# Diagonal score blocks of 384 and 128 columns joined into one of 512, in two attentions of a hybrid network

## The chip, the cores and the metric

The kernel runs on one core of one Trainium2 chip. The metric is the device time of one execution in microseconds (us). A core has five engines that run their own instruction queues side by side: PE (TensorE, matrix products; PEld is its weight load), DVE (VectorE), ACT (ScalarE), POOL (GpSimd) and SP (SyncE, which here only issues transfers). PE writes to PSUM, 8 banks of 512 fp32 columns on 128 partitions; DVE and ACT read from there, POOL works on SBUF only.

## The reference

Two layers of a residual network over x of shape 4 x 1024 x 128, all fp32. Layer 0: gated linear attention, a mixture of experts, causal attention, the mixture again. Layer 1: rotary attention without softmax, a dense network, ALiBi attention, the dense network again. The change touches the two softmax attentions alone. Both have 16 heads of 8 columns, and T = 1024:

```python
def _L0_attn_b_ref(x, Wq, Wk, Wv, Wo):          # causal; values have 64 columns a head
    q = (x @ Wq).reshape(B, T, 16, 8).transpose(0, 2, 1, 3)      # k alike, v with 64
    scores = jnp.einsum('bhqd,bhkd->bhqk', q, k) / sqrt(8)
    scores = jnp.where(causal, -jnp.inf, scores)
    attn = jax.nn.softmax(scores, axis=-1)
    ctx = jnp.einsum('bhqk,bhkd->bhqd', attn, v)
    return ctx.transpose(0, 2, 1, 3).reshape(B, T, 16 * 64) @ Wo
def _L1_attn_b_ref(x, W_attn, b_attn, W_proj, b_proj, temperature):   # ALiBi; values have 8
    att = jnp.einsum('bqhd,bkhd->bhqk', q, k) * scale / temperature
    att = att + jnp.where(causal, slopes * rel, -jnp.inf)
    w = jax.nn.softmax(att, axis=-1)
    return jnp.einsum('bhqk,bkhd->bqhd', w, v).reshape(B, T, 128) @ W_proj + b_proj
```

## The kernel before, in words

The layers follow each other: gated linear attention, experts, causal attention (from about 360 to 1330 us of the profile), experts, rotary attention and the first dense layer, ALiBi attention (about 1690 to 2340), the second dense layer.

Both attentions run through `softmax_attention` (from L786). A number `n` stands for a pair of heads of one batch item: the queries and keys of one head lie on partitions 0 to 63 and those of the other on 64 to 127 (`g` is 0 or 1), and the pair's products use the two halves of PE. There are 8 pairs in a batch item, 32 in all. `Pairs.load` brings a pair in with SP's transfers, `Pairs.product` (L722) multiplies queries and keys, and `Pairs.hide` (L728) adds a large negative triangle to a 128 x 128 block on the diagonal with two more matmuls.

**Maxima.** For every query the largest score is needed before the exponential. `Pairs.maxima` makes scores with queries on partitions, in tiles of 128 queries (`i`) by up to 512 keys (`c` is 0 or 1), one PSUM bank a head, and DVE reduces each: with the mask (L750, followed by the read of its accumulator) where the tile reaches the diagonal, plainly (L755) where it does not. The list `BY_QUERY` has twelve such steps for a pair. At the end `least` joins the halves, and `finish` turns it (L764), splits it into `nm_hi` and `nm_lo` (L766, L768), and writes them by transfers into two rows of the queries, so that the next scores come out with the maximum subtracted. This runs ahead of the rest by two pairs and six steps.

**Rounds, steps and turns.** The main loop takes two pairs a round, 16 rounds in an attention. In a round it goes through `BY_KEY`, twelve steps: for each half of the queries (`c`), the key tiles `j`, 4 for the first half and 8 for the second. In the last four key tiles of a half the block lies on the diagonal, and only 512, 384, 256 and 128 queries remain. A step has two turns, one for each pair. A turn makes the scores of both heads in one tile of two banks (L722, L728), takes their exponential on ACT into an `e` tile (L853), and then issues one step of the maxima, one part of the products of the step before, and one item of the queue `later` (`some()`). Every third turn it also issues one piece of what is put beside the attention (in the causal one the routing of the next mixture).

**Causal attention.** The products (L972) add into two banks `o0` and `o1`, one in each turn of a step, since the values have 64 columns. POOL adds the exponentials of all key tiles into the first one, `e_first` (L990). After the last key tile of a half, `consume` queues in `later`: the sums of `e_first` (L1002), four reciprocals (L1010), the scaling of both parts on POOL (L1016), an empty turn, and the projection (L936); the values of the next four heads come in between (L921). PSUM: 4 single banks, one scores tile of two banks, and `o0`, `o1`. There are four `e` tiles and four `e_first` tiles.

**ALiBi attention.** The products (L1198) add into one bank, all in the second turn of a step; a column of ones in the values gives the sums, so that POOL adds nothing. `later` gets an empty turn and the division (transposes L1212, then L1215 and L1216 on DVE). PSUM: 3 single banks, two scores tiles of two banks, and `o`.

All this goes through a scheduler that places every instruction in its engine's queue and sets the waits; each engine then works its queue in that order.

Of the kernel before, what the change touches and what calls it, by code (L numbers as in the profile page):

```python
# [13 lines left out]
F32 = mybir.dt.float32  # L14
# [624 lines left out]
class Pairs:  # L639
# [93 lines left out]
    def maxima(self, n, pool, steps):  # L733
# [5 lines left out]
        for i, c in steps:  # L739
            cols = min(512, (i + 1) * P - 512 * c)  # L740
            for g in range(2):
                ps = k.bank()
                self.product(
                    ps[:, :cols], n, g, slice(i * P, (i + 1) * P), slice(512 * c, 512 * c + cols),
                    "q", False,
                )
                to = nm[:, c, g, i : i + 1]
                if i < 4 * (c + 1):
                    junk = pool.tile([P, 512], F32, tag="junk", name="junk", bufs=1)
                    nc.vector.tensor_tensor_reduce(  # L750
                        junk[:, :cols], ps[:, :cols], self.mask[:, 512 - cols :], -1.0, 3e38,
                        ALU.add, ALU.min, to,
                    )
                else:
                    nc.vector.tensor_reduce(to, ps[:, :cols], AX.X, ALU.max, negate=True)  # L755
            yield
# [25 lines left out]
BY_QUERY = [(i, c) for i in range(NB) for c in range(i // 4 + 1)]  # L782
BY_KEY = [(c, j) for c in range(2) for j in range(4 * c + 4)]


def softmax_attention(  # L786
# [41 lines left out]
    for first in range(0, count, 2):  # L828
        if first % per == 0 and first // per + 1 < B:
            before(first // per + 1)  # L830
        if first % per == 2 and first // per + 1 < B:
            prologue(first // per + 1)
        for n in (first + 4, first + 5):
            if n < count:
                pairs.load(n)
        for c, j in BY_KEY:
            start = max(j * P, c * 512)
            w = (c + 1) * 512 - start
            es = []
            for i in range(2):  # L840
                n = first + i
                ps = ps_e.tile([P, 2, 512], F32, tag="scores", name="scores")
                for g in range(2):
                    pairs.product(
                        ps[:, g, :w], n, g, slice(start, start + w), slice(j * P, (j + 1) * P), "k", True,
                        j < 4 * c,
                    )
                if j >= 4 * c:
                    for g in range(2):
                        pairs.hide(ps[:, g, :P], g)  # L850
                tag = "e_first" if hold and j == 0 else "e"
                e = work.tile([P, 2, 512], F32, tag=tag, name=tag)
                power = nc.scalar.activation(e[:, :, :w], ps[:, :, :w], AF.Exp, scale=scale)  # L853
                k.mark = [power.ins.name]
                es.append(e)
                next(ahead, None)
                if late is not None:
                    later.extend(late[i]() or ())
                some()
                turn += 1  # L860
                if beside and turn % 3 == 0:
                    beside.popleft()()
            late = consume(first // per, first % per // 2, c, j, es)
# [8 lines left out]
def causal_attention(k: Core, pairs: Pairs, wq_d, wk_d, wv_d, wo_d, bring, after):  # L872
# [5 lines left out]
    with (  # L878
# [78 lines left out]
        def consume(b, r, c, j, es):  # L957
            skip = max(j - 4 * c, 0) * P
            if j == 0:
# [6 lines left out]
            end = j == 4 * c + 3  # L966
# [3 lines left out]
            def product(which):  # L970
                for i in range(4):
                    nc.tensor.matmul(  # L972
                        outs[which][32 * i : 32 * i + 32, skip:],
                        lhsT=v[:, j, i, 32 * which : 32 * which + 32],
                        rhs=es[i // 2][:, i % 2, : 512 - skip],
                        start=(j == 0), stop=end, skip_group_check=True,
                    )
# [6 lines left out]
            def second():  # L984
                product(1)

                if j:
                    for i in range(2):
                        to = total[i][:, :, skip:]
                        nc.gpsimd.tensor_add(to, to, es[i][:, :, : 512 - skip])  # L990
                if c == 0 and j == 0:
                    nb, nr = divmod(b * 4 + r + 1, 4)
                    if nb < B:
                        return values(nb, nr)
# [23 lines left out]
                todo = [sums, *(partial(invert, t) for t in range(4)), scaled, lambda: None]  # L1018
# [107 lines left out]
def alibi_attention(k: Core, pairs: Pairs, weights: AlibiWeights):  # L1126
# [3 lines left out]
    with (  # L1130
# [54 lines left out]
        def consume(b, r, c, j, es):  # L1185
            skip = max(j - 4 * c, 0) * P
            end = j == 4 * c + 3
            if j == 0:
# [7 lines left out]
            def second():  # L1196
                for i in range(4):
                    nc.tensor.matmul(  # L1198
                        o[32 * i : 32 * i + 32, skip:],
                        lhsT=v[:, j, 4 * r + i, :],  # L1200
                        rhs=es[i // 2][:, i % 2, : 512 - skip],
                        start=(j == 0), stop=end, skip_group_check=True,
                    )
# [578 lines left out]
```

## Time and profile before

| | |
|---|---|
| three runs | 2537.66, 2547.32, 2554.1 us; median 2547.32 |
| profiled execution | 2547.5 us; its span, from first to last instruction, 2545.8 us |
| granted PE clock, mean | 0.92 |
| causal attention, first to last exponential | 360.9 to 1299.2 us |
| ALiBi attention, first to last exponential | 1698.9 to 2326.3 us |
| exponentials (L853) | 704 + 64 into `e_first`, half in each attention |
| additions into `e_first` (L990) | 320, 541.1 us of POOL |
| masked and plain maxima (L750, L755) | 1024 and 512, 496.6 and 330.2 us of DVE |

A row of the timeline has the start, the length, the engine, the line and operation, what is written and from what, the shape, and how many equal instructions follow each other; in brackets stands how long the engine had been idle and what ended it. Matmuls overlap, so the length of one is more than the distance to the next. A row of the waits has who waited for whom, the time in total, how often, and the longest.

### The profile page before, as it was taken

How to read it: one execution, taken by the hardware profiler on the slowest of the kernel's cores; microseconds unless marked ns; L12 is line 12 of the kernel's file. 1: busy time of each engine (PE TensorE's matmuls, PEld its weight loads, DVE VectorE, ACT ScalarE, POOL GpSimd, SP SyncE). 2: the span in 40 equal slices, each digit the busy share in tenths (PEclk: the TensorE clock that was granted, in tenths of full speed). 3: DMA queues.
4: the chain of work that ended last, by engine and by line, in shares of the span. 5: the costliest groups of instructions: out<-in, count | busy, mean ns of one | idle time of the engine just before them, and what ended most of it. 6: DMA issues, size and time to landing. Idle time of an engine off the chain costs nothing. (4 is left out here: it accounts for less than half of the span.)

```text
span 2545.8 us, 39865 instructions
## 1 busy us (share of the span) xinstructions
PE 2252.5 (88%) x14101; PEld 1237.0 (49%) x14101; DVE 1664.2 (65%) x4795; ACT 1254.0 (49%) x2033; POOL 927.2 (36%) x722
## 2 busy tenths in 40 slices
PE   6785679999999989998984999989999999997998
PEld 4564533443434344443343666744445444444666
DVE  6978265767657766776334776476777767774544
ACT  6553214455444544553431566615555555555865
POOL 2212405677488748766752332311001000000222
PEclk8988769999889989998997999967999999998999
DMA  9300230200200120100033000402113131000000
GB/s 255 111 9 17 85 105 22 80 19 26 84 26 19 40 77 23 31 18 27 2 98 98 9 9 1 131 2 89 35 34 111 34 101 45 24 24 1 9 9 18
DMA packets 92391, 124.80 MB, mean 49 GB/s; under 512 B 13211, under 2 KB 66462, under 8 KB 92174
## 3 DMA queue, kind: packets, MB, share of 16 engines
q1 hardware_dynamic: 88862, 115.76, 16.0%
q0 software_dynamic: 2560, 5.30, 0.6%
q8 instruction: 120, 1.97, 0.3%
q10 hardware_dynamic: 752, 0.98, 0.1%
q14 instruction: 97, 0.79, 0.1%
HBM read 67.57 MB, written 52.85 MB: 47 GB/s over the span
## 5 line engine op out<-in xcount | busy, mean ns | idle before, releaser
L853 ACT ACTIVATE e<-scores 128x1024 f32<-128x1024 f32 (+3 forms) x704 | 545.3, 792 | 583.8 <-PE scores L728 295.0
L990 POOL TENSOR_TENSOR e_first<-e_first,e 128x1024 f32<-128x1024 f32 (+3 forms) x320 | 541.1, 1722 | 327.1 <-ACT e L853 261.4
L750 DVE CUSTOM_DVE_ANT_0 junk<-bank,mask 128x128 f32<-128x128 f32 (+3 forms) x1024 | 496.6, 485 | 202.7 <-PE bank L722 134.2
L755 DVE TENSOR_REDUCE nm<-bank 128x1 f32<-128x512 f32 x512 | 330.2, 680 | 146.6 <-PE bank L722 144.4
L972 PE MATMUL o<-e,v 128*32 128x512 f32 (+3 forms) x2560 | 305.7, 497 | 0.0
L722 PE MATMUL bank<-aa_k,aa_q 62*128 62x512 f32 (+3 forms) x768 | 244.6, 427 | 26.1 <-DVE nm L755 15.7
L722 PE MATMUL bank<-ca_k,ca_q 62*128 62x512 f32 (+3 forms) x768 | 191.1, 419 | 31.0 <-DMA ca_k<-ca_k 13.9
L1198 PE MATMUL o<-e,v 128*32 128x512 f32 (+3 forms) x1536 | 218.2, 514 | 0.0
L722 PE MATMUL scores<-ca_q,ca_k 64*128 64x512 f32 (+3 forms) x768 | 181.3, 444 | 27.7 <-ACT e L853 26.0
L722 PEld LDWEIGHTS scores<-ca_q,ca_k 64*128 64x128 f32 x768 | 78.0, 188 | 250.1 <-ACT e L853 157.5
L728 PE MATMUL scores<-halves 64*128 64x128 f32 x2048 | 199.2, 261 | 0.0
L728 PEld LDWEIGHTS scores<-halves 64*128 64x128 f32 x2048 | 192.2, 195 | 11.1 <-issue 3.9
L722 PE MATMUL scores<-aa_q,aa_k 64*128 64x512 f32 (+3 forms) x768 | 171.3, 415 | 4.8 <-ACT e L853 4.7
L722 PEld LDWEIGHTS bank<-aa_k,aa_q 62*128 62x128 f32 x768 | 119.0, 199 | 108.1 <-DVE nm L755 60.0
L1108 POOL TENSOR_TENSOR lo<-val,hi 128x512 fp32r<-128x512 f32 x16 | 20.2, 1278 | 391.8 <-ACT hi L1107 372.2
L1516 DVE TENSOR_TENSOR h<-val,h 128x512 fp32r<-128x512 f32 x128 | 90.9, 718 | 102.8 <-ACT h L1515 77.1
L1470 PE MATMUL bank<-h,ff_h1s 128*128 128x512 f32 x512 | 135.5, 409 | 15.4 <-POOL h L1464 10.5
L1460 POOL CAST h<-gate 128x512 fp32r<-128x512 f32 x32 | 26.7, 834 | 333.2 <-DVE gate L1493 323.5
L722 PEld LDWEIGHTS scores<-aa_q,aa_k 64*128 64x128 f32 x768 | 80.2, 192 | 138.5 <-ACT e L853 63.9
L1010 DVE RECIPROCAL raw<-raw 128x128 f32<-128x128 f32 x128 | 117.6, 935 | 44.2 <-ACT raw L1006 44.2
L722 PEld LDWEIGHTS bank<-ca_k,ca_q 62*128 62x128 f32 x768 | 94.6, 200 | 99.5 <-issue 38.6
L1510 ACT ACTIVATE val<-bank,ff_t 128x512 f32<-128x512 f32 x128 | 88.2, 689 | 84.4 <-PE bank L1470 73.9
(291 smaller groups left out, 3716.6 us busy)
## 6 DMA issues: line engine op xcount, KB each, us to landing
aa_q<-aa_q SPq DMA_DIRECT2D x64, 208.0 KB
ca_q<-ca_q SPq DMA_DIRECT2D x64, 128.0 KB
ca_k<-ca_k SPq DMA_DIRECT2D x64, 128.0 KB
aa_k<-aa_k SPq DMA_DIRECT2D x64, 128.0 KB
wi<-in_moe_wi_dram SPq DMA_DIRECT2D x16, 256.0 KB
wo<-in_moe_wo_dram SPq DMA_DIRECT2D x16, 256.0 KB
back<-blank SPq DMA_DIRECT2D x8, 512.0 KB
got<-back SPq DMA_DIRECT2D x8, 512.0 KB
```

Of the source, the lines that this page charges most:

```text
L722: self.k.nc.tensor.matmul(out, lhsT=lhsT, rhs=rhs, start=True, stop=stop, skip_group_check=True)
L728: self.k.nc.tensor.matmul(ps, lhsT=part[:, 0, :], rhs=part[:, 1, :], start=False, stop=(a == 1), skip_group_check=True,)
L750: nc.vector.tensor_tensor_reduce(junk[:, :cols], ps[:, :cols], self.mask[:, 512 - cols :], -1.0, 3e38, ALU.add, ALU.min, to,)
L755: nc.vector.tensor_reduce(to, ps[:, :cols], AX.X, ALU.max, negate=True)
L853: power = nc.scalar.activation(e[:, :, :w], ps[:, :, :w], AF.Exp, scale=scale)
L972: nc.tensor.matmul(outs[which][32 * i : 32 * i + 32, skip:], lhsT=v[:, j, i, 32 * which : 32 * which + 32], rhs=es[i // 2][:, i % 2, : 512 ...
L990: nc.gpsimd.tensor_add(to, to, es[i][:, :, : 512 - skip])
L1010: nc.vector.reciprocal(part, part)
L1198: nc.tensor.matmul(o[32 * i : 32 * i + 32, skip:], lhsT=v[:, j, 4 * r + i, :], rhs=es[i // 2][:, i % 2, : 512 - skip], start=(j == 0), sto ...
L1470: nc.tensor.matmul(ps, lhsT=weights[:, c, :], rhs=inputs[c][i], start=(s == 0), stop=(s == len(steps) - 1))
L1510: nc.scalar.activation(val, ps, AF.Gelu, scale=s[:, o : o + 1])
L1516: nc.vector.tensor_sub(nxt[1][:, o, :], val, hi.bitcast(F32))
```

## The change

The lists of steps are rewritten. In the main loop the key tiles with 384 and 128 queries (the second and fourth of a diagonal) become one step: both blocks lie side by side in one scores tile, 512 columns a head, and one exponential covers them. The tile with 256 queries comes before them. A round has ten steps (20 turns) instead of twelve (24). In the maxima the tiles with 128 and 384 keys are joined alike, in one bank, and a pair has ten steps instead of twelve; both banks of a step are now asked for before the first matmul. The products, the additions on POOL and the maxima on DVE are still issued once for each block. The queue `later` gives two items in a turn while more than eight wait, and between the scaling and the projection stand two empty turns instead of one.

```diff
@@ Pairs.maxima
-        for i, c in steps:
-            cols = min(512, (i + 1) * P - 512 * c)
+        for c, several in steps:
+            parts, at = [], 0
+            for i in several:
+                cols = min(512, (i + 1) * P - 512 * c)
+                parts.append((i, cols, slice(at, at + cols)))
+                at += cols
+            banks = [k.bank() for _ in range(2)]
+            for i, cols, place in parts:
+                for g in range(2):
+                    self.product(
+                        banks[g][:, place], n, g, slice(i * P, (i + 1) * P), slice(512 * c, 512 * c + cols),
+                        "q", False,
+                    )
             for g in range(2):
-                ps = k.bank()
-                self.product(ps[:, :cols], n, g, ...)
-                to = nm[:, c, g, i : i + 1]
-                ... (one masked or plain reduction)
+                for i, cols, place in parts:
+                    to, ps = nm[:, c, g, i : i + 1], banks[g][:, place]
+                    ... (the same reduction, of ps)
             yield
@@
-BY_QUERY = [(i, c) for i in range(NB) for c in range(i // 4 + 1)]
-BY_KEY = [(c, j) for c in range(2) for j in range(4 * c + 4)]
+BY_QUERY = [
+    *((0, i) for i in ((0, 2), (1,), (3,), (4,), (5,), (6,), (7,))),
+    *((1, i) for i in ((4, 6), (5,), (7,))),
+]
+BY_KEY = [(c, j) for c in range(2) for j in [*((j,) for j in range(4 * c + 1)), (4 * c + 2,), (4 * c + 1, 4 * c + 3)]]
@@ softmax_attention
-        for c, j in BY_KEY:
-            start = max(j * P, c * 512)
-            w = (c + 1) * 512 - start
+        for c, several in BY_KEY:
+            parts, w = [], 0
+            for j in several:
+                skip = max(j - 4 * c, 0) * P
+                parts.append((j, skip, slice(w, w + 512 - skip)))
+                w += 512 - skip
...
-                for g in range(2):
-                    pairs.product(ps[:, g, :w], n, g, slice(start, start + w), ...)
-                if j >= 4 * c:
-                    for g in range(2):
-                        pairs.hide(ps[:, g, :P], g)
+                for j, skip, place in parts:
+                    for g in range(2):
+                        pairs.product(
+                            ps[:, g, place], n, g, slice(c * 512 + skip, (c + 1) * 512),
+                            slice(j * P, (j + 1) * P), "k", True, j < 4 * c,
+                        )
+                    if j >= 4 * c:
+                        for g in range(2):
+                            pairs.hide(ps[:, g, place.start : place.start + P], g)
...
-                some()
+                some(2 if len(later) > 8 else 1)
...
-            late = consume(first // per, first % per // 2, c, j, es)
+            late = consume(first // per, first % per // 2, c, parts, es)
@@ causal_attention, consume
             def product(which):
-                for i in range(4):
-                    nc.tensor.matmul(..., rhs=es[i // 2][:, i % 2, : 512 - skip], start=(j == 0), stop=end, ...)
+                for j, skip, place in parts:
+                    for i in range(4):
+                        nc.tensor.matmul(
+                            ..., rhs=es[i // 2][:, i % 2, place], start=(j == 0), stop=(j == 4 * c + 3), ...
+                        )
...
-                if j:
-                    for i in range(2):
-                        to = total[i][:, :, skip:]
-                        nc.gpsimd.tensor_add(to, to, es[i][:, :, : 512 - skip])
+                for i in range(2):
+                    for j, skip, place in parts:
+                        if j:
+                            to = total[i][:, :, skip:]
+                            nc.gpsimd.tensor_add(to, to, es[i][:, :, place])
...
-                todo = [sums, *(partial(invert, t) for t in range(4)), scaled, lambda: None]
+                todo = [sums, *(partial(invert, t) for t in range(4)), scaled, lambda: None, lambda: None]
@@ alibi_attention, consume: second() loops over parts in the same way
```

## The prediction

> **What bounds the kernel now.** I read the windows of the two attentions first, then the engines' timelines inside one undisturbed round of each, then the waits. The page gives the time of this execution and its fullest engine; the windows stand in pairs, one round and the whole attention, first the causal one, then ALiBi (columns: stretch, its length, PE, PEld, DVE, ACT, POOL busy, granted clock, DMA).
>
> ```profile
> span 2545.8 us, 39865 instructions
> PE 2252.5 (88%) x14101; PEld 1237.0 (49%) x14101; DVE 1664.2 (65%) x4795; ACT 1254.0 (49%) x2033; POOL 927.2 (36%) x722
> ```
>
> ```profile
> 783.30:832.40 49.10, 48.73 (x401) 21.12 (x398) 35.25 (x104) 24.73 (x37) 38.60 (x26) 1.00 0.06 17
> 360.90:1299.20 938.30, 883.67 (x6369) 377.83 (x6369) 601.98 (x1740) 440.58 (x658) 639.44 (x407) 0.94 0.12 34
> 2121.20:2157.50 36.30, 34.48 (x268) 17.24 (x266) 27.09 (x90) 19.75 (x28) 0.00 (x0) 1.00 0.17 39
> 1698.90:2326.30 627.40, 596.79 (x4375) 305.42 (x4377) 441.09 (x1435) 334.68 (x477) 19.73 (x14) 0.95 0.19 51
> ```
>
> ACT, whose instructions the change removes, is about half busy in both. The causal round has two parts. From the sums' end (787.0) to the end of the product that reads e_first in the second half (806.3), 19.3 us, PE's blocks follow each other without a gap. From there POOL runs without a gap until it has added everything the next sums need:
>
> ```profile
> 806.36 16.39 POOL L990 TENSOR_TENSOR e_first<-e_first,e 128x1024 f32<-128x1024 f32 x7 [5.65 <-ACT e L853]
> 822.70 2.52 POOL L1016 TENSOR_TENSOR ctx<-raw 128x512 f32<-128x512 f32 x2
> 825.16 8.41 POOL L990 TENSOR_TENSOR e_first<-e_first,e 128x1024 f32<-128x1024 f32 x5
> ```
>
> The sums already feel it; they take 1.74 us where POOL is last and 1.04 where it isn't (PE's timeline):
>
> ```profile
> 785.31 1.74 PE L1002 MATMUL bank<-e_first,ones 128*32 128x512 f32 x8
> ...
> 811.35 1.04 PE L1002 MATMUL bank<-e_first,ones 128*32 128x512 f32 x8
> ```
>
> In the ALiBi round POOL does nothing. PE and DVE hold each other through three PSUM banks: over that attention (first two rows) DVE waits 98.6 us for maxima matmuls; the third row, from the waits of the causal one, is the price of late POOL additions.
>
> ```profile
> DVE nm L755 <- PE bank L722: 69.3, 78, 2.7
> DVE junk L750 <- PE bank L722: 29.3, 56, 1.2
> ACT e L853 <- POOL e_first L990: 82.0, 37, 5.0
> ```
>
> **The change, part by part.** Durations are starts to next starts in the timelines of these rounds, clock 1.00.
>
> *Fewer exponentials.* ACT goes from 24 to 20 exponentials in each of 32 rounds, 128 fewer. The groups by form give the fixed part: 1026 ns for 1024 columns and 384 for 256 make 642 ns for 768, so 170 ns without columns; 128 x 0.17 = 21.8 us of ACT. It lies beside PE and DVE, so I count nothing; were ACT the bound it would be -22.
>
> ```profile
> L853 ACT ACTIVATE e<-scores 128x1024 f32<-128x1024 f32 x320 | 319.0, 1026 | 218.8 <-PE scores L722 111.8 <-PE scores L728 82.8 <-POOL e_first L990 21.8
> ...
> L853 ACT ACTIVATE e<-scores 128x256 f32<-128x256 f32 x128 | 49.0, 384 | 143.1 <-PE scores L728 70.9 <-PE bank L722 49.6 <-POOL e_first L990 21.9
> ```
>
> *PE, DVE, POOL and SP issue the same instructions*; in the order of the built program only ACT's count changes. A scores or maxima block of two matmuls takes 0.34, 0.28, 0.22, 0.16 us at 512, 384, 256, 128 columns, hides 0.17, so 384 and 128 cost 0.44 apart or together. What changes is who waits.
>
> *ALiBi.* A step (two turns) lasts as long as the longer of its PE and its DVE work. DVE takes per maxima (both heads) 1.21 us plain, masked 0.87, 1.15, 1.42, 1.68 at 128, 256, 384, 512, so 2.29 for a merged pair; finishing adds 0.59, dividing 0.54. PE takes per step its blocks, plus the product of the step before: 1.00, 0.78, 0.57, 0.36 by columns. Where a maxima matmul stands inside a product, the product costs twice:
>
> ```profile
> 2139.34 0.28 PE L722 MATMUL bank<-aa_k,aa_q 62*128 62x256 f32 x1
> 2139.55 1.05 PE L1198 MATMUL o<-e,v 128*32 128x512 f32 x2
> 2140.53 0.38 PE L722 MATMUL bank<-aa_k,aa_q 62*128 62x256 f32 x1
> 2140.84 1.06 PE L1198 MATMUL o<-e,v 128*32 128x512 f32 x6
> ```
>
> There are 44 such cuts before and 43 after, three a round. Before, the longer of PE and DVE over the twelve steps: 2.36, 3.20, 2.89, 2.61 | 3.10, 4.20, 3.28, 3.40, 2.89, 2.61, 3.10, 2.08 = 35.7, against 36.3 measured. After, over ten: 3.50, 3.37, 4.03 | 2.89, 3.90, 3.50, 3.26, 4.03, 2.89, 2.66 = 34.0, all but two of them (3.90, 3.26) DVE's or within 0.3 of it. The 4.03 of keys 4, for one: a merged pair 2.29, a 256 one 1.15 and finishing 0.59 on DVE, against PE's 3.98 (scores and hides 1.0, maxima 0.6, transpose and second maxima 0.4, a cut product 1.98). That is -1.7 us a round, for 15 rounds (the last has no maxima) **-26**. Bounds: DVE without its waits for PE is 36.3 - 7.3 (its idle rows in that round) = 29.0 and PE's own after is 29.3, so I take half of the 98.6, -50, as the best; if a bank held for two reductions (1.15 instead of 0.6 us) eats it all, 0. One page speaks against sharing a bank: the Trainium skill, "PSUM — Partial Sum Buffer", Terms, says that TensorE may not write a bank while another engine reads it. Before has one piece per bank, so no row shows that; by it the first reduction starts a 384 block later, which the 1.7 would not notice while DVE has work.
>
> *Causal, PE's part.* Same matmuls, 19.1 us by my sum, plus two waits. The scores have one buffer here, so a turn lasts at least blocks + 0.27 to ACT + exponential 1.02 + 0.08 back. For the merged step that is 0.78 + 1.37 = 2.15, against PE's 1.79 and 2.11 in the two turns: +0.4. DVE has 14.3 us in the five turns after the sums (merged 2.29 twice, the wide ones, four reciprocals of 0.95 popped two a turn) against PE's 10.3; four banks lend two turns, and PE waits 1.3 where it waited 0.5 before: +0.8. So +1.2 x 16 = **+19**; bounds 0 (queue as even as before) and +2 x 16 = +32.
>
> *Causal, POOL's part.* Before 2 x (4 x 2.37 + 1.83 + 1.28 + 0.74) + 2.5 = 29.2; after the same sum in another order. So 0 either way, and this is where the causal gain goes: POOL does not see the merging.
>
> *The smaller ones.* Cut products fall in the causal attention from 19 to 10 at 512, rise from 3 to 11 at 384, fall by 8 at narrower ones: -9 x 0.98 + 8 x 0.78 - 4 x 0.57 - 4 x 0.36 = **-6** (0 if other work hides it). The second empty turn lets the projection (L936) wait less for the scaling queued on POOL: at best the 6.4 us PE waits there, half taken, **-3**; without cover the next scores queue behind it and lose the same. Before each loop DVE does 26 maxima instead of 30, but the six extra ones weigh 8.8 instead of 7.2 us, twice: **+3** (0 to +3). SP's loads are moved by no more than a turn, and ALiBi shows no wait of maxima for them.
>
> Sum: -26 + 19 - 6 - 3 + 3 = -13, on this execution's 2547.5 us (span 2545.8 and 1.7 around it; the median of the runs, 2547.32, is 0.2 less): **2534.5**. With its own bounds 2515 to 2560.
>
> **Rivals.** *The sums halve the clock (slower).* After, the last additions are 5.2 us (384 and 128 for both) instead of 1.5, so they cannot be done early. By the chain from 806.3, POOL ends 29.4 us on as before, but PE, with 3.9 us of values, sums and projection left there instead of 5, reaches the second half of the sums at 27.8: idle 1.7 us, where the row at 785.31 shows 0.7. Gaps and the clock after them, from PE's timeline and the windows:
>
> ```profile
> 1247.02 1.04 PE L1002 MATMUL bank<-e_first,ones 128*32 128x512 f32 x2 [1.41 <-POOL e_first L990]
> ...
> 895.69 1.35 PE L90 MATMUL bank<-ident,xn 128*128 128x128 f32 x5 [1.58 <-DVE xn L125]
> ```
>
> ```profile
> 1246.00:1256.00 10.00, 8.98 (x62) 3.47 (x64) 3.39 (x4) 4.81 (x8) 5.43 (x6) 1.00 0.00 1
> 895.60:906.00 10.40, 10.15 (x21) 4.52 (x22) 3.81 (x11) 3.52 (x5) 1.80 (x1) 0.57 0.04 10
> ```
>
> After 1.41 us the clock held; after 1.58 it was 0.57 for 10.4 us, 4.5 us lost. From about 1.5 us this decides: 16 x 4.5 = +72, 2534.5 + 72 = **2607**. Against it: before's 0.7 was 1.3 by the same chain, so 1.7 may be 1.1. The Trainium skill, "TensorE: Matmul & The Clock Gate", Part 1, lets the clock fall after a whole idle window of about 3.4 us; by it these gaps cost nothing and the sum stays as it was. The row at 895.69 disagrees, and I go by the row.
>
> *ALiBi gives nothing.* The lockstep is one of latencies, not of work: -26 becomes 0, **2560.5**. For it: the cuts remain, and PE waits for DVE in the same step as DVE for PE. Against: my rule gives 35.7 for 36.3.
>
> *More than forecast.* ALiBi -50, and the causal waits 0 instead of +19 because exponentials late for POOL (82.0) find more work per buffer: 2547.5 - 50 - 6 - 3 + 3 = **2491.5**. Against it: DVE would need all its idle time.
>
> That the change does not do what it says is out: merged blocks stand together in the built order, and exponentials are 640 instead of 768.
>
> **How the numbers follow.** Forecast 0.32, clock 0.28, ALiBi nothing 0.18, more 0.22. Predicted 2534.5. The range takes in the better rival whole and most of the way to the clock one (half its rounds would be 2571): 2488 to 2595. Within 1% is 2522 to 2573 (some 25 us either side, about what a measurement here tells from no change). Faster: 0.22 and 0.04 of the forecast = 0.26; slower: 0.28 and 0.02 of the one without ALiBi gain, less 0.02 where few rounds halve = 0.28; within: 0.46.
>
> **What would show it.** ALiBi's window 601 instead of 627, an undisturbed round 34.6 instead of 36.3, DVE's waits for maxima below 70; exponentials x640. Causal window 950 instead of 938, its quiet round 50 instead of 49, POOL without a gap from T0 (the 806.3 above) to the sums, and about the same 639 us busy. Wrong if the causal attention gets shorter by over 10 us (POOL was not the bound), if ALiBi's round stays at 36 (the rule of the longer engine fails), or if the causal clock falls below 0.94 (the rival).

## The result and the profile after

The changed kernel takes 2548.95 us (median of 20 runs, 2543.25 to 2563.09) against 2542.86 for the kernel before (20 runs): 1.0035 times as long, 95% interval 1.0021 to 1.0050. By these intervals it is slower by some 5 to 13 us, where 13 less were forecast (the two medians alone lie 6 apart). The time lies inside the forecast's range, 14 above the forecast.

The page of the changed kernel: exponentials, and so ACT's instructions, are 128 fewer (1905 for 2033); PE's and DVE's counts are the same.

```profile
PE 2226.5 (87%) x14101; PEld 1244.2 (49%) x14101; DVE 1688.0 (66%) x4795; ACT 1245.1 (49%) x1905; POOL 929.9 (36%) x722
```

The windows, in the order of the forecast's: a causal round, the causal attention, an ALiBi round, the ALiBi attention.

```profile
782.30:833.20 50.90, 49.48 (x402) 22.46 (x403) 35.93 (x107) 24.53 (x33) 39.27 (x25) 1.00 0.06 17
362.30:1296.90 934.60, 871.38 (x6351) 386.51 (x6351) 619.13 (x1740) 435.92 (x594) 640.15 (x404) 0.94 0.12 34
2127.10:2162.90 35.80, 32.83 (x268) 16.79 (x266) 27.54 (x90) 19.45 (x24) 0.00 (x0) 1.00 0.17 41
1703.30:2328.10 624.80, 578.79 (x4369) 299.58 (x4368) 445.62 (x1430) 330.56 (x413) 19.77 (x14) 0.94 0.19 51
```

ALiBi's 624.8 stands against 627.4 before and 601 forecast; the rounds without a load stayed at 36. The causal round went from 49.1 to 50.9 (forecast 50). The causal attention is shorter by 3.7 in this execution, but it starts 1.4 later, and its work after the last exponential is 4.2 us longer: the last sums have to wait for POOL, PE alone for 2.39 of them.

```profile
1301.44 1.05 PE L1016 MATMUL bank<-e_first,ones 128*32 128x512 f32 x4 [2.39 <-POOL e_first L1004]
```

POOL's chain in the causal round (timeline of POOL). As forecast it has no gap from T0, the 808.22, to the sums, and T0 to the next sums is as long as before (27.94 us, 27.96 before). But T0 itself is later in the round: POOL stood 6.66 us ahead of it, where it stood 5.65 before, and from the start of the sums to T0 it is 22.96 us instead of 21.05. That is the whole growth of the round.

```profile
808.22 11.70 POOL L1004 TENSOR_TENSOR e_first<-e_first,e 128x1024 f32<-128x1024 f32 x5 [6.66 <-PE o L985]
819.88 2.52 POOL L1030 TENSOR_TENSOR ctx<-raw 128x512 f32<-128x512 f32 x2
822.36 13.88 POOL L1004 TENSOR_TENSOR e_first<-e_first,e 128x1024 f32<-128x1024 f32 x8
```

Of these 1.9 us, 1.1 lie between the end of the sums and T0. PE's timeline shows two pieces of values (x8) right ahead of the product that T0 waits for, and one more stands before them at 801.80; before there were two in all, at 800.88 and 803.60.

```profile
804.42 1.99 PE L934 MATMUL bank<-ca_wv,xnT 128*128 128x256 f32 x8
...
807.01 1.06 PE L985 MATMUL o<-e_first,v 128*32 128x512 f32 x8
```

The other 0.8 lie in the sums, which take 2.5 us to the next block on PE instead of 1.7: they come in two halves, with 0.49 us of idle time between them. The clock stays at 1.00. So the rival of the halved clock did not come about in these rounds.

```profile
785.26 1.03 PE L1016 MATMUL bank<-e_first,ones 128*32 128x512 f32 x4
786.77 1.05 PE L1016 MATMUL bank<-e_first,ones 128*32 128x512 f32 x4 [0.49 <-POOL e_first L1004]
```

The waits in ALiBi's window. DVE waits 99.1 us for maxima matmuls, as long as before (98.6), where under 70 was to show the forecast right. PE's weight loads wait 71.4 us for masked maxima, where it was 23.6; for plain ones they wait less (29.0, it was 53.7), so that together 77.3 us have become 100.4.

```profile
PEld bank L722 <- DVE nm L757: 71.4, 116, 1.0
DVE junk L757 <- PE bank L722: 52.8, 68, 2.3
DVE nm L761 <- PE bank L722: 46.3, 66, 1.8
```

### The profile page after: what moved, and what is told of

Read it like the earlier page. It is cut to its first block, busy times and chain, and to the rows that moved or that the text cites. A ratio compares the mean times of both kernels' runs of the same rounds, so it can differ in the third digit from the quotient of the medians.

```text
span 2547.7 us, 39417 instructions
## 1 busy us (share of the span) xinstructions
PE 2226.5 (87%) x14101; PEld 1244.2 (49%) x14101; DVE 1688.0 (66%) x4795; ACT 1245.1 (49%) x1905; POOL 929.9 (36%) x722
## 5 line engine op out<-in xcount | busy, mean ns | idle before, releaser
L866 ACT ACTIVATE e<-scores 128x1024 f32<-128x1024 f32 (+1 forms) x576 | 526.8, 929 | 549.8 <-PE scores L728 375.3
L1004 POOL TENSOR_TENSOR e_first<-e_first,e 128x1024 f32<-128x1024 f32 (+2 forms) x320 | 544.5, 1725 | 348.3 <-PE o L985 206.3
L985 PE MATMUL o<-e,v 128*32 128x512 f32 (+3 forms) x2560 | 290.3, 494 | 0.0
L722 PE MATMUL bank<-aa_k,aa_q 62*128 62x512 f32 (+3 forms) x768 | 220.8, 427 | 41.1 <-DVE nm L757 26.4
L722 PE MATMUL bank<-ca_k,ca_q 62*128 62x512 f32 (+3 forms) x768 | 208.8, 425 | 37.1 <-DMA ca_k<-ca_k 14.2
L1212 PE MATMUL o<-e,v 128*32 128x512 f32 (+3 forms) x1536 | 214.8, 521 | 0.1
L728 PE MATMUL scores<-halves 64*128 64x128 f32 x2048 | 193.3, 259 | 0.0
L722 PEld LDWEIGHTS bank<-aa_k,aa_q 62*128 62x128 f32 x768 | 111.3, 202 | 124.9 <-DVE nm L757 80.9
L722 PE MATMUL scores<-aa_q,aa_k 64*128 64x512 f32 (+3 forms) x768 | 166.0, 416 | 0.8 <-ACT e L866 0.8
L722 PEld LDWEIGHTS bank<-ca_k,ca_q 62*128 62x128 f32 x768 | 103.5, 202 | 125.9 <-DVE nm L757 55.0
```

The source lines that it names most:

```text
L722: self.k.nc.tensor.matmul(out, lhsT=lhsT, rhs=rhs, start=True, stop=stop, skip_group_check=True)
L728: self.k.nc.tensor.matmul(ps, lhsT=part[:, 0, :], rhs=part[:, 1, :], start=False, stop=(a == 1), skip_group_check=True,)
L985: nc.tensor.matmul(outs[which][32 * i : 32 * i + 32, skip:], lhsT=v[:, j, i, 32 * which : 32 * which + 32], rhs=es[i // 2][:, i % 2, place ...
L1004: nc.gpsimd.tensor_add(to, to, es[i][:, :, place])
L1212: nc.tensor.matmul(o[32 * i : 32 * i + 32, skip:], lhsT=v[:, j, 4 * r + i, :], rhs=es[i // 2][:, i % 2, place], start=(j == 0), stop=(j == ...
```

## The experiments

All of them use the changed code with lists and queue rule as parameters of each attention. With the twelve one-element steps, one empty turn and one item a turn it gives the kernel before again.

```diff
+OLD_QUERY = [(c, (i,)) for i in range(NB) for c in range(i // 4 + 1)]
+OLD_KEY = [(c, (j,)) for c in range(2) for j in range(4 * c + 4)]
-    for _ in range(len(BY_QUERY) * 2 + 6):
+    for _ in range(len(queries) * 2 + 6):
-        for c, several in BY_KEY:
+        for c, several in keys:
```

Ratios below are to the kernel before, run beside each group of experiments, with 95% intervals. Windows are first to last exponential of an attention in one profiled execution. "Quiet round" is one without the loading of the next batch item, clock 1.00.

### Which attention loses

**The change in the causal attention alone** (`keys=BY_KEY` there, `keys=OLD_KEY` in ALiBi).

> The new lists, the faster queue and the second empty turn in the causal attention alone; ALiBi keeps twelve steps. Theory (the causal attention gained nothing, and pays at its ends: +1.4 us ahead of it, +4.2 after its last exponential, about -4 between): total +2 to +9 us on before, ratio 1.001 to 1.0035, ALiBi's window 627. Rival (ALiBi carries the loss of the medians, and its profiled -2.6 was chance): total within 2 us of before. Rival (the causal attention itself gains, as its profiled window of 934.6 for 938.3 has it): total -2 to -4.

1.0043 (1.0021 to 1.0064), 2550.97 us: all of the loss, about 11 us, a little more than the theory's 2 to 9; both rivals fall. Quiet rounds 50.5 to 52.6 (49.0 before), ALiBi's window 627.9. The seven quiet rounds together are 16 us longer than in the kernel of the next experiment, whose causal attention is that of before; the rounds with loads are shorter in this profile.

**The change in ALiBi alone.**

> The new lists in ALiBi alone; the causal attention is that of before. Theory (ten steps save ACT, which was not the bound, and nothing of PE): ALiBi's window 623 to 627, quiet round 36.2, total 0 to -3 us, ratio 0.999 to 1.000. Rival (the profile of the change understates a gain, forecast -26): window about 601, ratio 0.990. Rival (the shared bank, held for two reductions, costs more than the steps save): ratio above 1.002.

0.9992 (0.9968 to 1.0016). Quiet rounds 35.8 (36 before), window 618.9 in this execution, below the theory's 623 to 627. In the ratio the theory holds: by its times ALiBi with ten steps can't be told from ALiBi with twelve. The two ratios together give the whole change.

### ALiBi: the cut products

**Products ahead of the maxima, ten steps.**

```diff
-                next(ahead, None)
+                if hold:
+                    next(ahead, None)
                 if late is not None:
                     later.extend(late[i]() or ())
+                if not hold:
+                    next(ahead, None)
```

> As the kernel with the new lists in ALiBi alone, but in ALiBi's turns the products of the step before are issued ahead of the maxima, so that hardly any product is cut by a maxima matmul (5 instead of 43; maxima matmuls come up to 1 us later). Theory (PE's order with its cut products sets the round, 0.98 us each): 38 x 0.98 = -37 at most, ALiBi's window 590 to 608, ratio 0.986 to 0.994. Rival (the latency from matmul through three banks to DVE and back sets it): the later maxima cost as much as the cuts, window 620 to 635. Rival (DVE's work sets it): window unchanged, 623 to 627.

0.9866 (0.9834 to 0.9897), 2507.15 us: 33 us less than before, as the theory of the cuts had it, and the best quiet rounds take 33.7 instead of 35.8. The window of the profiled execution (the longest of its six) is 601.9.

**The same with twelve steps.**

> The kernel before (twelve steps in both attentions), but with ALiBi's products ahead of the maxima: 17 cut products instead of 43. Theory of the cuts: 26 x 0.98 = -25 at most, window 602 to 615, ratio 0.990 to 0.996; with twelve steps less is gained than with ten, since the forecast's rule of the longer engine gives 35.7 there and 34.0 here. Rival (latency through the banks): window 620 to 640, ratio 0.998 to 1.005. If this gains as much as the kernel with ten steps, the merging itself is worth nothing in ALiBi even without cuts.

0.9994 (0.9973 to 1.0014), a miss. Quiet rounds do fall from 36 to 34.2, but rounds with loads become longer in exchange (43.1 and 47.5 in the profile, one at a clock of 0.76, where five profiles with the unchanged ALiBi have 35.8 to 36.1 and 45.1 to 45.5). Moving the product is not the same as not cutting it, and 17 cuts remain, so a cleaner pair was needed.

**Whole products without moving them.** An order that needs no semaphore is laid from the step's last maxima matmul to the product; hardly a product is cut any more.

```diff
+                        made = nc.tensor.matmul(   # the product, L1212
...
+                        tc.add_manual_dep(
+                            made.ins, pairs.latest,    # the last matmul of Pairs.product
+                            mybir.DependencyInfo(mybir.DependencyClass.NoSync, mybir.DependencyReason.SCHED_ONLY),
+                        )
```

> The new lists in ALiBi alone; the maxima stay ahead of the products as in the change, but an order (without a semaphore) is laid from the step's last maxima matmul to the four matmuls of the product, so that no product is cut. Theory A (the cut itself costs, 0.98 us each, about three a round): window about 600 as with the products issued first, quiet round 33.7 to 34.5, ratio on before 0.985 to 0.990. Theory B (what paid was that the product no longer stands behind maxima matmuls that wait for a bank): nothing of it, since the product waits for both maxima matmuls now: quiet round 35.5 to 37, ratio 0.998 to 1.004.

0.9840 (0.9807 to 0.9873), 2499.6 us, 41 less than before. Theory A holds and B falls: the product still stands behind both maxima matmuls, and that costs nothing. The windows, a quiet round and the whole ALiBi attention, first with cuts (ten steps in ALiBi alone), then without:

```profile
2113.82:2149.67 35.85, 32.88 (x268) 16.81 (x266) 27.53 (x90) 19.46 (x25) 0.00 (x0) 1.00 0.17 39
1695.90:2314.80 618.90, 573.46 (x4369) 297.22 (x4368) 445.66 (x1431) 330.27 (x413) 19.77 (x14) 0.95 0.19 51
```

```profile
2094.16:2127.63 33.47, 30.09 (x268) 16.50 (x266) 27.50 (x90) 19.45 (x24) 0.00 (x0) 1.00 0.18 42
1698.20:2286.20 588.00, 535.59 (x4369) 294.94 (x4368) 445.29 (x1430) 330.27 (x413) 19.79 (x14) 0.94 0.20 54
```

The same instructions, 2.4 us a round less. PE's busy time falls by 2.8 (32.88 to 30.09: three cuts of 0.98 are 2.9). DVE's timeline of the same two rounds shows where the cuts were paid. First the round with cuts: from PE's timeline the last three quarters of a cut product and the maxima matmuls that come behind it, then four of DVE's eight waits for PE, those at the cuts and right behind them:

```profile
2141.80 1.06 PE L1215 MATMUL o<-e,v 128*32 128x512 f32 x6
...
2143.18 0.45 PE L722 MATMUL bank<-aa_k,aa_q 62*128 62x512 f32 x2
```

```profile
2130.49 0.69 DVE L761 TENSOR_REDUCE nm<-bank 128x1 f32<-128x512 f32 x1 [0.52 <-PE bank L722]
2132.15 1.29 DVE L761 TENSOR_REDUCE nm<-bank 128x1 f32<-128x512 f32 x2 [0.96 <-PE bank L722]
2139.25 0.29 DVE L757 CUSTOM_DVE_ANT_0 junk<-bank,mask 128x128 f32<-128x128 f32 x1 [0.89 <-PE bank L722]
2143.66 0.69 DVE L757 CUSTOM_DVE_ANT_0 junk<-bank,mask 128x512 f32<-128x512 f32 x1 [1.32 <-PE bank L722]
```

Without cuts two of the four are left:

```profile
2111.43 1.29 DVE L763 TENSOR_REDUCE nm<-bank 128x1 f32<-128x512 f32 x2 [0.49 <-PE bank L722]
2121.66 0.69 DVE L759 CUSTOM_DVE_ANT_0 junk<-bank,mask 128x512 f32<-128x512 f32 x1 [0.66 <-PE bank L722]
```

These four waits fall from 3.69 us to 1.15, by 2.5, as much as the round; the other four are the same within 0.04 us each. Only the first of them is for the matmul that does the cutting. In the other three DVE has done with that one, runs out of work while PE is still at the rest of the product or at the scores after it, and waits for the maxima matmuls behind them.

Over the whole attention, DVE's waits for maxima matmuls fall below the 70 that the forecast had asked for (waits in these windows, with cuts and without):

```profile
DVE junk L757 <- PE bank L722: 50.9, 67, 1.8
DVE nm L761 <- PE bank L722: 42.7, 65, 1.8
```

```profile
DVE junk L759 <- PE bank L722: 31.8, 57, 2.0
DVE nm L763 <- PE bank L722: 28.8, 50, 1.8
```

From 93.6 to 60.6 they fall by 33.0; the window falls by 30.9. Since DVE's busy time is the same in both (445.66 and 445.29), what the window loses has to leave DVE's idle time; that it leaves these waits, and in the round the ones at the cuts, is what the rows add.

**Whole products with twelve steps.** The same order in the kernel before.

> The kernel before, twelve steps everywhere, with the order that keeps ALiBi's products whole (1 cut instead of 43). Theory (a cut costs its 0.98 us where PE is last in a step, which with twelve steps is fewer steps: the forecast's rule has DVE ahead in about half of them): quiet round 34 to 34.5, 10 to 22 us below before, ratio 0.991 to 0.996, so that the merged steps are worth the 20 to 30 us that lie between this and 0.984. Rival (the cuts alone were the loss and ten steps bring nothing of their own): ratio 0.982 to 0.986, as with ten steps.

0.9913 (0.9881 to 0.9946): 22 us less than before. Its interval does not meet that of the ten steps. The quiet round (window) is 35.0, with 1.5 more than ten steps have:

```profile
2081.39:2116.37 34.98, 32.10 (x268) 16.70 (x266) 27.00 (x90) 19.79 (x28) 0.00 (x0) 1.00 0.18 41
```

So the merging is worth 0.7% here, about 18 us, once the products are whole, and 2 us while they are cut, less than the interval. The rival, that the cuts were the whole story, falls.

**Less work for DVE, with cuts.** The masked full tiles are reduced over their last 256 columns only.

```diff
                         junk = pool.tile([P, 512], F32, tag="junk", name="junk", bufs=1)
+                        if len(steps) == 10 and i == 4 * c + 3:
+                            ps, cols = ps[:, 256:], 256
```

> The new lists in ALiBi alone with the cut products as they are, but DVE reduces only the last 256 of the 512 columns of the two full masked tiles of a pair (part of the maxima is left out): 0.53 us less four times a round, 2.1 us of DVE. Theory (with the cuts PE's order sets the round, and DVE's work does not): ALiBi's quiet round 35 to 35.9 instead of 35.8, total 0 to -12 us on before, ratio 0.995 to 1.000. Rival (DVE sets eight of ten steps, as the forecast had it): quiet round 33.7 to 34.2, ratio 0.987 to 0.991.

0.9941 (0.9908 to 0.9974), quiet round 35.3: of 2.1 us that DVE no longer works, 0.5 reach the round, as the theory had it (the ratio lies a little below its range). The rest turned into waiting: DVE's waits for maxima matmuls in ALiBi are 120.7 now (71.6 for masked and 49.1 for plain ones) instead of 93.6.

**Less work for DVE, products first.** The two edits together.

> ALiBi with ten steps, products ahead of the maxima and 2.1 us of DVE less a round (only the last 256 columns of the full masked tiles reduced; part of the maxima is left out). Theory (without cuts the forecast's rule holds, and DVE sets most steps): quiet round 33.7 down to 31.9 to 32.7, 15 to 27 us below the kernel with the products first, ratio on before 0.976 to 0.981. Rival (PE's queue still sets it): quiet round 33.2 to 33.7, 0 to -8 us, ratio 0.984 to 0.987.

0.9822 (0.9792 to 0.9852), quiet round 32.6 instead of 33.7: half of the 2.1 us reach the round, twice as much as with cuts. That is the upper edge of what the theory had for the round, and in the ratio it lies between theory and rival. Without cuts DVE carries more of the round than with them, but not all of it, as the forecast's rule would have it.

### The causal attention: the queue

**The queue alone, twelve steps** (`some(2 if len(later) > 8 else 1)` and the second empty turn).

> The kernel before with only the queue changed: two items a turn while more than eight wait, and the second empty turn; twelve steps in both attentions. Theory (the loss comes from the merged scores): nothing, total -2 to +3 us on before, ratio 0.999 to 1.001. Rival (the quicker queue puts values ahead of the product that POOL waits for, and reciprocals in pairs on DVE, and this is the loss): +8 to +12, ratio 1.003 to 1.005.

1.0106 (1.0076 to 1.0136): 27 us slower, more than the whole change. My theory fell; the rival, which I had put at 8 to 12, was right in kind and too small. Quiet rounds are 51.9 instead of 49.0.

**The quicker queue without the second empty turn.**

> The kernel before with the quicker queue alone (two items a turn while more than eight wait); one empty turn, twelve steps. Theory (the quicker queue brings the second half's sums three turns earlier, into the turn with the last values, and its projection five turns earlier, behind a scaling that stands in POOL's queue behind additions): it carries all of the 27 us of the queue experiment or more, +24 to +32 us on before, ratio 1.009 to 1.0125. Rival (the second empty turn is what costs): 0 to +5 us.

1.0097 (1.0072 to 1.0122): it is the quicker queue. POOL's timeline of one quiet round shows how:

```profile
531.32 9.39 POOL L1007 TENSOR_TENSOR e_first<-e_first,e 128x1024 f32<-128x1024 f32 x4 [8.62 <-ACT e L869]
```

POOL stands idle for 8.62 us in the middle of the round; it was 5.65 before. It may not add into the second half's `e_first` until both products have read it, nor before the exponential to be added is there (the one the row names); both stand behind the same work on PE. By PE's timeline the quicker queue puts all four pieces of values and the sums (1.0 us each) ahead of the second of these products, where two pieces stood before: 3 x 1.0. POOL's idle time ahead of T0 is 2.97 longer, and the round 2.9. So the size is the theory's, and the place is T0 more than the projection that it named.

**Merged maxima alone, and merged scores alone** (both with the new queue; the second issues two maxima steps in a merged turn).

> The causal attention has the merged maxima (ten steps in 24 turns) and the new queue, but twelve steps of scores; ALiBi as before. Theory: DVE's merged pair of 2.29 us and four banks cost little, -2 to +3 us on before, ratio 0.999 to 1.001. Rival (a bank held for two reductions holds PE): +6 to +12, 1.0025 to 1.005.

1.0093 (1.0063 to 1.0124), outside both ranges, since the queue's cost is in it. Against the queue's 1.0106 the merged maxima make 3 us, less than the intervals.

> The causal attention has the merged scores (ten steps, 20 turns) and the new queue, but the old twelve steps of maxima, two of them in each merged turn; ALiBi as before. Theory (one buffer of scores makes a merged turn 2.15 us, and the last additions on POOL come late at every half, worst at the attention's end): +6 to +12 us on before, ratio 1.002 to 1.005, quiet round 50 to 51, last additions 4 us after the last exponential's products as with the whole change. Rival (the maxima are what costs): total within 3 us of before.

1.0279 (1.0248 to 1.0311), a miss that tells little: two maxima steps in one turn are a load of their own, and the quiet rounds are 52 to 58 long. It does not isolate the scores. From the other runs: the whole change in the causal attention is 1.0043 and its queue alone 1.0106, so that with ten steps the quicker queue costs about 16 us less than with twelve.

**One empty turn instead of two, with everything else of the change.**

> The whole change in the causal attention, but one empty turn before the projection instead of two; ALiBi as before. Theory (the projection waits for the scaling on POOL, so an earlier one costs): +2 to +8 us on the kernel with two empty turns, ratio on before 1.005 to 1.0075; the forecast had 3 us for the second empty turn. Rival (the empty turn does nothing): ratio 1.0035 to 1.005.

1.0038 (1.0019 to 1.0057) against 1.0043: the theory falls, the rival holds. The second empty turn does nothing that can be measured.

**Fewer additions on POOL.**

```diff
-                        if j:
+                        if j and j != 4 * c + 3:
```

> As the kernel with the whole change in the causal attention alone, but POOL's additions of the last key tile of each half (128 queries, 0.74 us a tile) are left out, so the sums lack these exponentials: 64 additions, 47 us of POOL, 3.0 us a round fewer. Theory (POOL sets the second half of a round, without a gap from T0 to the sums): quiet round from 50.7 to 48 to 49.5, total 25 to 45 us below the kernel with the whole change in the causal attention, ratio on before 0.987 to 0.994. Rival (PE's queue sets it and POOL follows): quiet round 50 to 50.7, total 0 to -8 below it, ratio 1.001 to 1.004.

0.9969 (0.9947 to 0.9991), 19 us below the whole causal change; quiet rounds 49.2 to 50.8, the shortest 49.2 to 49.5, where they were 50.5 to 52.6. Of the 3.0 us a round that POOL is spared, 1.2 to 1.3 reach the round. POOL's timeline shows where the other half went: the idle time ahead of T0 grows from 6.66 to 8.31, since there PE sets the time.

```profile
746.03 11.71 POOL L1007 TENSOR_TENSOR e_first<-e_first,e 128x1024 f32<-128x1024 f32 x5 [8.31 <-PE o L988]
```

So neither theory nor rival as I had put them: POOL sets the half after T0, PE the half before.

**A queue spread out, ten steps.**

```diff
-                some(2 if len(later) > 8 else 1)
+                some(2 if len(later) > (12 if hold else 8) else 1)
                 def invert(t):
-                    part = raw[:, 2, t * P : (t + 1) * P]
-                    nc.vector.reciprocal(part, part)
+                    for at in (t, t + 1):
+                        part = raw[:, 2, at * P : (at + 1) * P]
+                        nc.vector.reciprocal(part, part)
-                todo = [sums, *(partial(invert, t) for t in range(4)), scaled, lambda: None, lambda: None]
+                todo = [sums, partial(invert, 0), partial(invert, 2), scaled, lambda: None, lambda: None]
```

> The causal attention with the new lists of steps, but its queue spread out: reciprocals two to an item, two empty turns, and two items a turn only above twelve waiting. The sums of the second half come then where they were in the kernel before, the values at most one a turn. Theory (the merged steps save 16 us, and the quicker queue costs 27 of them): -10 to -18 us on before, ratio 0.993 to 0.996, quiet round 48 to 49. Rival (with ten steps there is no room, whatever the queue): within 4 us of the kernel with the whole change in the causal attention, ratio 1.003 to 1.006.

0.9993 (0.9971 to 1.0014): the loss is gone, and the interval does not meet the 1.0021 to 1.0064 of the quicker queue with the same ten steps. So the queue is what made the causal attention slower. But the 10 to 18 us of gain did not come. In the round of 48.7 at 782 us POOL's idle time ahead of T0 is 5.80 (5.65 before, 6.66 with the change). The profile has rounds of 48.7 (forecast by the theory), but also rounds of 51.8, 53.6 and 56.3 in the same attention, with a clock of 0.93, 0.94 and 0.91. In the one of 53.6 the sums waited 0.67 us for POOL; the clock is 0.50 from 743.1 to 746.5, some 9 us behind that, and again from 770.4 to 773.8, after PE waited 0.90 us for DVE (to 769.29). What lowers the clock was not tried by itself and stays open.

**Whole products in the causal attention**, with ten steps and the spread queue, and with twelve steps and the old queue.

> The causal attention with the new lists, the spread queue, and the order that keeps products whole: 5 cut products instead of 41; ALiBi as before. Theory (a cut costs up to 0.98 us, half of these lie where PE sets the time, the other half beside POOL): 10 to 20 us below the spread queue alone, ratio on before 0.991 to 0.995. Rival (POOL sets the round from T0 on and takes whatever PE saves): 0 to -4, ratio 0.9975 to 1.000.

> The kernel before with twelve steps everywhere and its own queue; only the order that keeps the causal attention's products whole is added (21 cut instead of 54). Theory (as for the kernel with ten steps, with fewer cuts left out): 8 to 20 us below before, ratio 0.992 to 0.997. Rival (POOL takes it): 0 to -4. If this and its partner with ten steps come out alike, the merged steps are worth nothing in the causal attention even with a good queue; by the theory ten steps are 5 to 15 us better.

0.9999 (0.9981 to 1.0018) and 1.0003 (0.9984 to 1.0022): nothing, where the same order was worth 22 us (twelve steps) and 39 (ten) in ALiBi. And since the two come out alike, the merged steps are worth nothing measurable in the causal attention, even with a queue that costs nothing. The quiet round with twelve steps is 49.0 as before. In the quiet causal rounds of before hardly a product is cut (one of 128 columns in the round of the forecast's windows); nearly all cuts lie in the other rounds, and taking them away there did not show in the time.

### Both together

The new lists in both attentions, the spread queue, and whole products everywhere.

> The new lists in both attentions, the causal queue spread out (reciprocals in pairs, two items a turn only above twelve), and the order that keeps products whole in both. Theory (the two attentions add): ALiBi's -41 and the causal -3 to 0, ratio on before 0.982 to 0.986, some 2495 to 2503 us, 45 to 55 us below the kernel as changed. Rival (the gains in the clock's spells don't add): 0.987 to 0.990.

0.9835 (0.9802 to 0.9869), 2501.24 us, with ALiBi's window at 587.0: some 48 us below the kernel as changed and as good as the ten steps in ALiBi alone (0.9840). It is faster than both kernels; all of the gain is ALiBi's.

## Why the prediction was wrong, point by point

**ALiBi, -26: the step that failed.** The sum put a step at the longer of its PE and DVE work, and counted a cut, in the step of keys 4, as part of PE's 3.98 us, covered by DVE's 4.03. In the round with cuts that is shown above this step takes 4.60 us (2138.18 to 2142.78). In it DVE waits 0.89 for PE and PE 0.37 for DVE, so it is longer than the work of either; and the cut product puts off the maxima matmuls behind it, for which DVE then waits 1.32. The product and these matmuls share PE's queue, so the cut adds to DVE's time and does not lie beside it. The runs show it in three ways: without cuts the waits of DVE at these places fall by 2.5 us a round and the round by 2.4; with cuts, DVE spared 2.1 us passes on 0.5; and the quiet round without cuts is 33.5, where the rule had 34.0 with them. The rival "ALiBi gives nothing" was right, and its reason ("the cuts remain") too. I gave it 0.18 because the rule's 35.7 agreed with 36.3 measured, in one round; that agreement did not test what a cut costs beside a busier DVE.

**Causal, PE's part +19 and POOL's part 0: near in sum by luck.** The causal terms of the sum made +12 or so (19 - 6 - 3 and a part of the +3), and the attention lost 11. But these terms do not hold one by one. POOL's chain "from T0 to the sums" is unchanged, as the forecast said (27.94 and 27.96). The sum did not ask whether T0 moves: it comes 1.9 later after the start of the sums, 0.8 by the sums' wait and 1.1 because two items a turn bring a third piece of values onto PE ahead of the product that T0 waits for. These terms were not in the sum; with twelve steps the quicker queue costs 27 us. Of the two waits of PE that made the +19 one was the price of the merged turn, the other of reciprocals popped two a turn, with 0 as the bound for a queue as even as before. With the spread queue, where the merged steps remain, the loss is gone (0.9993): that bound was right, and the price of the merged turn does not show. Nor did the round's growth come 16 times: the seven quiet rounds are 1.5 to 3.7 us longer, 16 us in all, and the others are shorter in the profile. Why the quicker queue costs 16 us less with ten steps than with twelve stays open.

**The halved clock (0.28).** The sums wait 0.5 us in the round shown, not 1.7, and the clock is 1.00 there. In the quiet round that begins at 970 us they wait 1.52, about the 1.5 from which this rival was to decide, and the clock stays at 1.00 for more than 100 us:

```profile
975.76 1.05 PE L1016 MATMUL bank<-e_first,ones 128*32 128x512 f32 x4 [1.52 <-POOL e_first L1004]
```

With the spread queue, on the other hand, waits of 0.90 us were followed by 3.4 us at 0.50 (from 770.4 and from 1012.7). So the length of a single wait does not decide, and the forecast's two rows (1.41 and 1.58) were too few for the threshold that it took from them.

**Cut products -6.** Nothing: whole products are worth nothing measurable in the causal attention.

**Second empty turn -3.** Nothing, by two pairs of runs (1.0038 and 1.0043, 1.0097 and 1.0106).

**Maxima ahead, +3.** From the first maxima matmul to the first exponential the causal attention takes 0.9 us longer (29.1 for 28.3), ALiBi no longer (27.6 for 27.9): about +1, inside the bounds of 0 to +3.

**Not in the sum:** the end of the causal attention, +4.2 us by the profile, where the last additions of 5.2 us (the rival had their length) have nothing to hide behind.

**ACT -21.8, counted 0.** The exponentials' busy time falls by 19.7 us (470.3 for the three forms to 450.6) and brings nothing that can be measured, as forecast. The forecast's 642 ns are the difference of the two forms, which lie 768 columns apart; an exponential of 768 columns takes 811, and 811 + 384 - 1026 gives the same 170 ns.

## What to carry to other kernels

Before you count a piece of work as covered by another engine, ask whether it stands ahead, in its own queue, of the instruction that this engine will wait for next: then it can add, however well the busy times fit. When a list gets shorter and a queue beside it is made quicker to keep up, follow the instructions that the quicker queue puts ahead of the one that releases the bound engine; here that cost 27 us with twelve steps, and the merging brought nothing measurable beside it. And where an order written out by a scheduler splits a group of matmuls, an order laid by hand that needs no semaphore can be worth more than the change in hand.

## What the runs showed of the hardware

A product here is four matmuls (eight records in the timeline), one for each group of 32 columns of PE, and all four together take 1.0 us; one of them alone, with a matmul of another shape behind it, takes the same (the timeline of before has 0.98 from its start to the maxima matmul's, and 1.06 for the other three). So a foreign matmul inside the group costs a whole product. The Trainium skill, "TensorEngine Tiling (Array Packing)", Key Properties, says that tiles work independently, and that a change of the tiling mode drains the engine first; these rows agree with both, though no run here sets the two apart, and the pair of runs in ALiBi gives the price: about 0.8 us of the 0.98 for each of three cuts a round with ten steps (35.85 to 33.47).
